# Where the weights of a decoder's first feed-forward are made ternary: in the cross-attention, or earlier, in the self-attention

## The chip, the cores and the metric

The kernel runs on one core of a Trainium2 chip. The metric is the device time of one execution in microseconds (us), the median of several runs. Five engines matter: PE (TensorE, the matrix multiplier, with its weight loads shown apart as PEld), DVE (VectorE), ACT (ScalarE), POOL (GpSimd), and SP (SyncE, which here only issues DMAs). Each works through its own queue in order: an instruction that waits holds up all that stand behind it on the same engine.

## The reference

Two decoder layers over x of shape (4, 512, 512), batch by batch. Each has a self-attention, a cross-attention and a feed-forward, and each of the six is followed by a sum with its input and a layer norm. What the change touches is the weight side of the first feed-forward:

```python
def weight_quant(w):
    scale = 1.0 / jnp.clip(jnp.mean(jnp.abs(w)), EPS)
    wq = jnp.clip(jnp.round(w * scale), -1.0, 1.0) / scale
    return w + jax.lax.stop_gradient(wq - w)
...
gate = bitlinear(x, w_gate)
up = bitlinear(x, w_up)
intermediate = jax.nn.silu(gate) * up
return h_bitlinear(intermediate, w_down)
```

So every weight becomes -1, 0 or 1 times a mean of absolute values over the whole matrix. That mean has to be known before the first weight can be rounded: each matrix (1 M weights, 4 MB) is read twice.

## The kernel before, in words

The six blocks are called A (self-attention), B (cross-attention), C (feed-forward) of layer 0, and D, E, F of layer 1; each has four batches, A0 to A3 and so on. `lanes` (L1254) runs two of them side by side: it takes one step of each in turn, and starts the next one when the last has said "next" and a lane is free. After each such round it gives one step to work in the background (`BESIDE`, L40): key C0 (`l0_ffn_scales`, L543) from the start of A1 to that of B0, key C (`l0_ffn_weights`, L575) from the start of B0 to that of B3. What the background hasn't done when a block needs it is done there at once (`need`, L1247).

`Pipe` (L43) puts an instruction off by some steps: `pipe.later(3, f)` calls f at the third `pipe.tick()` from now. The program is written in the order of these steps, and the framework's scheduler makes of it one queue for each engine: in the order of the code where nothing has to wait, ahead of it where an instruction is ready before others. `issue_after(ins)` (as in L557) keeps what is written under it behind `ins` on the queue of that instruction's engine; it is no wait at run time.

Buffers in SBUF are tiles of 128 partitions x 2 KB, in rings: O with 69 slots (most operands that live long: the high and low halves of the split float32 matrices, the exponentials, the ternary weights `tb`), T with 13, X with 12, W with 4 (weights on their way in, `tw`). PSUM has 8 banks.

**A (L330).** For each batch, q and k are projected (8 groups of 12 matmuls, "qk"), ACT adds the bias (`evac`, L340), DVE and POOL turn them by the rotary angles (`turn`, L349 and L352; `join`, L357), and they are split into a high and a low half (`split`, L137: the high one on ACT, L143, the low one on DVE or POOL, L146). Meanwhile the x of the next batch is loaded transposed and split, with the low halves `xTl` on POOL (`load_pairs`, L258). Then come v, the scores ("as"), the softmax, the transposes and the product with v ("pv"). POOL adds the bias row `bvo` to the four tiles of x (L408), which are needed only at the end, at L425.

**B (L457).** Per batch 16 steps. A step takes two heads: 6 matmuls for scores (L526), a row maximum on DVE (L474), an exponential on ACT (L476), a norm on POOL (L482), and six steps later 8 transposes (L248), copies (L489), and 4 matmuls into the output (L498).

**C0, beside A.** For each of the three matrices (`wg_t`, `wu_t`, `wd_t`) 16 chunks of 128x512 are loaded (256 KB each) and DVE sums their absolute values (`absum`, L558). A matmul adds these up over the partitions (L569), and L571 and L572 make the mean and the scale.

**C, beside B.** All 48 chunks are loaded again. For each, DVE does two instructions, `quant`: scale and add a large constant, which rounds (L587), and clip (L588). ACT then takes the constant off and writes bfloat16 (`put`, L596), two chunks to one tile `tb` of O. Gate and up come first, column group by column group, then down. From there C's matmuls (L687, L689, L741) read them.

Of the kernel before, what the change touches and what calls it, by code (L numbers as in the profile page):

```python
# [10 lines left out]
F32 = mybir.dt.float32  # L11
F32R = mybir.dt.float32r
F16 = mybir.dt.float16
BF16 = mybir.dt.bfloat16
I32 = mybir.dt.int32
U8 = mybir.dt.uint8
AF = mybir.ActivationFunctionType
ALU = mybir.AluOpType
AX = mybir.AxisListType
PSUM = bass.MemoryType.PSUM  # L20

B, S, D = 4, 512, 512
P = 128
NT = 4
MAGIC = 12582912.0
# [17 lines left out]
class Pipe:  # L43


    def __init__(self):
        self.todo = []
# [21 lines left out]
class Net:  # L69
    def __init__(self, ctx, tc, args):  # L70
        self.tc = tc
        self.nc = tc.nc
        self.a = args
        self.n = 0
        pool = lambda name, **kw: ctx.enter_context(tc.tile_pool(name=name, **kw))
        self.const = pool("const", bufs=1)
        self.op = pool("op", bufs=O_BUFS)
        self.tp = pool("tp", bufs=T_BUFS)
        self.xp = pool("xp", bufs=X_BUFS)
        self.wp_ = pool("wp", bufs=W_BUFS)  # L80
        self.small = pool("small", bufs=4)
        self.psum = pool("psum", bufs=8, space=PSUM)
        nc = self.nc
        tc.keep_in_program_order(nc.scalar.preload_act_table_set(LOG_EXP))
        self.ident = self.c("ident", [P, P])
        make_identity(nc, self.ident)
        self.ident16 = self.c("ident16", [P, P], BF16)
        nc.vector.tensor_copy(self.ident16, self.ident)
        self.ones = self.c("ones", [P, P])
        nc.gpsimd.memset(self.ones, 1.0)  # L90
        scratch = lambda name, shape: nc.dram_tensor(name, shape, F32, kind="Internal").ap()
        self.had_scratch = scratch("had_scratch", (2, NT, 2048, P))
        self.gu_codes = scratch("gu_codes", (22, P, 512))
        self.xd = [args["x"]] + [scratch(f"x{i}", (B, S, D)) for i in range(1, 6)] + [args["out"]]
        self.bg, self.table, self.emitted, self.piece, self.since = {}, None, {}, {}, {}

        self.low, self.stacked = {}, None
        self.gu, self.dn = {}, []
        self.pre = {}
        self.w1 = {}  # L100
        self.mean, self.scale = {}, {}
        self.tern = {name: {} for name in self.TERNARY}
# [227 lines left out]
    def l0_attn(self, b):  # L330
        nc, a = self.nc, self.a
        pipe = Pipe()
# [4 lines left out]

        def evac(ps, w, m):
            z = zs[w, m] = self.t("z")
            nc.scalar.activation(z, ps, AF.Identity, bias=self.qkb[:, w * NT + m : w * NT + m + 1], scale=1.0 if w else P ** -0.5)  # L340
            if m % 2:
                pipe.later(1, turn, w, zs[w, m - 1], z)

# [16 lines left out]
        for w in range(2):  # L360
            for m in range(NT):
                pipe.tick()
                ps = self.pa("qk")
                self.mm3(ps, [(self.cols(self.wqk[w][k], slice(m * P, (m + 1) * P)), xT[k]) for k in range(NT)])
                pipe.later(1, evac, ps, w, m)
                yield
            if b == 0 and w == 0:
                self.l0_attn_bv()
                yield from self.l0_attn_wvo(pipe)
# [16 lines left out]
        with self.tc.issue_after(self.pre.pop(("x", b)).ins):  # L386
            x = self.load_x(0, b)
# [4 lines left out]
        q, k = qk  # L392
        joined = self.joined
# [9 lines left out]
        for i in range(NT):  # L403
            pipe.tick()
            ps = self.pa("as")
            self.mm3(ps, [(self.cols(q[m], slice(i * P, (i + 1) * P)), k[m]) for m in range(NT)])
            with self.tc.issue_after(joined.ins):
                nc.gpsimd.tensor_tensor(x[i], x[i], self.bvo, ALU.add)  # L408
            pipe.later(1, soft, ps, i)
            yield  # L410
# [129 lines left out]
        w = self.a[name]  # L540
        return [(k, c, w[k * P : (k + 1) * P, c * 512 : (c + 1) * 512]) for c in range(w.shape[1] // 512) for k in range(w.shape[0] // P)]

    def l0_ffn_scales(self):  # L543

        nc = self.nc
        self.had = self.c("had", [P, P], F32R)
        self.had16 = self.load(self.c("had16", [P, P]), self.a["had16"])
        f = self.t("had")
        nc.gpsimd.dma_start(f[:, 0:P], self.a["had"])
        pipe = Pipe()  # L550
        pipe.later(3, nc.vector.tensor_copy, self.had, f[:, 0:P])
        for name in self.TERNARY:
            chunks = self.ternary_chunks(name)
            part = self.c(name + "_abs", [P, len(chunks)])

            def absum(f, n):
                with self.tc.issue_after(self.mark.ins):  # L557
                    nc.vector.tensor_reduce(part[:, n : n + 1], f, AX.X, ALU.add, apply_absolute_value=True)  # L558

            for n, (k, c, ap) in enumerate(chunks):  # L560
                pipe.tick()
                pipe.later(1, absum, self.load(self.w("tw"), ap), n)
                yield
            yield from pipe.drain()
            m = self.c(name + "_mean", [P, 4])
            nc.vector.tensor_reduce(m[:, 2:3], part, AX.X, ALU.add)
            yield
            ps = self.pb("tot")
            nc.tensor.matmul(ps[:, 0:1], self.ones, m[:, 2:3], start=True, stop=True)  # L569
            yield  # L570
            nc.vector.tensor_scalar(m[:, 0:1], ps[:, 0:1], 1.0 / (len(chunks) * P * 512), 1e-5, ALU.mult, ALU.max)  # L571
            nc.vector.reciprocal(m[:, 1:2], m[:, 0:1])  # L572
            self.mean[name], self.scale[name] = m[:, 0:1], m[:, 1:2]

    def l0_ffn_weights(self):  # L575

        nc = self.nc
        yield from self.bg["C0"]
        pipe = Pipe()
        order = [("wg_t", x) for x in self.ternary_chunks("wg_t")]  # L580
        up = [("wu_t", x) for x in self.ternary_chunks("wu_t")]
        order = [e for c in range(4) for e in order[4 * c : 4 * c + 4] + up[4 * c : 4 * c + 4]]
        order += [("wd_t", x) for x in self.ternary_chunks("wd_t")]
        cur = []

        def quant(name, k, c, f):
            nc.vector.tensor_scalar(f, f, self.scale[name], MAGIC, ALU.mult, ALU.add)  # L587
            nc.vector.tensor_scalar(f, f, MAGIC + 1.0, MAGIC - 1.0, ALU.min, ALU.max)  # L588
            pipe.later(1, put, name, k, c, f)

        def put(name, k, c, f):
            if not cur:
                cur.append(self.o("tb", BF16, 1024))
            o = cur[0][:, 0:512] if len(cur) == 1 else cur[0][:, 512:1024]
            cur.append(o)
            nc.scalar.activation(o, f, AF.Copy, bias=-MAGIC)  # L596
            self.tern[name][k, c] = o
            if len(cur) == 3:
                cur.clear()

        for name, (k, c, ap) in order:
            pipe.tick()
            pipe.later(1, quant, name, k, c, self.load(self.w("tw"), ap))
            yield
        yield from pipe.drain()

# [674 lines left out]
def body(tc, args, phases=range(6)):  # L1281
    with ExitStack() as ctx:
        net = Net(ctx, tc, args)
        net.gamma = net.load(net.c("gamma", [P, 1]), args["gamma"].to_broadcast([P, 1]))
        if 0 in phases:
            net.l0_attn_weights()
        net.bg = {("B", 0): net.l0_xattn_ctx(0), "C0": net.l0_ffn_scales(), "C": net.l0_ffn_weights(), "D": net.l1_attn_weights(), "F0": net.l1_ffn_codes(), "F": net.l1_ffn_weights()}
        f = [net.l0_attn, net.l0_xattn, net.l0_ffn, net.l1_attn, net.l1_xattn, net.l1_ffn]
        plain = ORDER.replace("+", "").replace("!", "").split()
        order = ORDER.split() if len(phases) == 6 else ["ABCDEF"[p] + str(b) for p in phases for b in range(B)]  # L1290

        def step(n):
            if len(phases) == 6:
                for first, last, key in BESIDE:
                    if plain.index(first) < n <= plain.index(last) + 1:
                        next(net.bg[key], None)

        def start(name):
            return f["ABCDEF".index(name[0])](int(name[1]))

        lanes(order, start, step)
# [68 lines left out]
```

## Time and profile before

| | us |
|---|---|
| three runs, median (lowest to highest) | 1584.54 (1584.25 to 1585.16) |
| the profiled execution, its own time | 1581.65 |
| its span, first to last instruction | 1580.0 |
| A, until B's first scores | 0 to 242.5 |
| B's scores, 64 steps | 242.5 to 445.5 |
| C, from its first gate matmul | from 461.6 |
| the loads of `tw` for C0 and C | 22.8 to 399.4 |
| `quant` on DVE | 229.8 to 409.4 |

| stretch, us | PE busy | DVE | ACT | POOL | DMA share |
|---|---|---|---|---|---|
| 0 to 242 | 233.8 | 161.9 | 93.1 | 144.1 | 0.43 |
| 242 to 461 | 212.6 | 201.3 | 182.5 | 112.4 | 0.38 |
| 461 to 765 | 293.2 | 231.8 | 240.9 | 98.9 | 0.50 |

How to read it: the first table says when each block runs, the second how long each engine was busy in these stretches (the third row is C). Matmuls are pipelined and their ends are modelled, so PE's figure is an upper one. The profile also has a list of groups of instructions, by line, engine and tile, with the busy time, the mean time of one in ns, and what ended the idle time before them; lists of who waited for whom; and the chain of work that ended last: from the last instruction it goes back, at each step to what released it or to the instruction before it on its engine.

### The profile page before, as it was taken

How to read it: one execution, taken by the hardware profiler on the slowest of the kernel's cores; microseconds unless marked ns; L12 is line 12 of the kernel's file. 1: busy time of each engine (PE TensorE's matmuls, PEld its weight loads, DVE VectorE, ACT ScalarE, POOL GpSimd, SP SyncE). 2: the span in 40 equal slices, each digit the busy share in tenths (PEclk: the TensorE clock that was granted, in tenths of full speed). 3: DMA queues.
4: the chain of work that ended last, by engine and by line, in shares of the span. 5: the costliest groups of instructions: out<-in, count | busy, mean ns of one | idle time of the engine just before them, and what ended most of it. 6: DMA issues, size and time to landing. Idle time of an engine off the chain costs nothing.

```text
span 1580.0 us, 25595 instructions
## 1 busy us (share of the span) xinstructions
PE 1515.4 (96%) x8222; PEld 1090.1 (69%) x8222; DVE 1232.9 (78%) x2658; ACT 1021.3 (65%) x2208; POOL 666.2 (42%) x672
## 2 busy tenths in 40 slices
PE   8999999999999999899999999999999999999996
PEld 6888786444544674477777668777687777777875
DVE  6486589999976688777577797767786888888896
ACT  5333336988878877888696864969634445545554
POOL 6673663555535303430435323353225344344342
PEclk9999999999999999999999999999999999999998
DMA  7043344455214744653434445633436630020101
GB/s 255 29 157 124 113 154 132 149 173 176 78 48 123 224 137 133 201 185 134 134 102 118 104 141 148 171 97 92 125 123 222 233 110 12 24 81 1 54 1 53
DMA packets 134150, 192.31 MB, mean 122 GB/s; under 512 B 17265, under 2 KB 52081, under 8 KB 134017
## 3 DMA queue, kind: packets, MB, share of 16 engines
q1 hardware_dynamic: 129888, 182.23, 36.3%
q0 software_dynamic: 4128, 8.46, 2.2%
q8 instruction: 65, 1.06, 0.3%
q14 instruction: 69, 0.56, 0.1%
HBM read 117.75 MB, written 47.71 MB: 105 GB/s over the span
## 4 chain that ended last, share of the span: by engine, by line
PE 63%; DVE 17%; ACT 8%; issue 6%; DMA 3%; POOL 3%; SPq 0%; ACTq 0%; DVEq 0%; POOLq 0%
PE fg L1185 7%; PE facc L1168 5%; PE dT L933 3%; DVE fg L1141 3%; PE pg L687 3%; PE had L755 2%; PE dn L741 2%; DVE bsm L474 2%; PE pu L689 2%; ACT de L923 2%; PE bo L498 2%; PE do L953 2%; PE qk L156 2%; PE qk L155 2%; PE qk L154 2%
## 5 line engine op out<-in xcount | busy, mean ns | idle before, releaser
L1141 DVE SCALAR_TENSOR_TENSOR fg<-fg,gs,fg 128x512 f32<-128x512 f32 x220 | 163.2, 745 | 30.9 <-ACT fg L1133 15.3
L923 ACT ACTIVATE de<-de,dm 128x128 f32<-128x128 f32 (+3 forms) x256 | 142.9, 563 | 11.3 <-DVE dm L919 10.9
L1185 PE MATMUL fg<-fxh,gu 128*128 128x512 f32 x352 | 140.2, 398 | 6.1 <-DVE fg L1141 3.1
L919 DVE CUSTOM_DVE_ANT_0 de<-ds,negm,thr 128x128 f32<-128x128 f32 (+3 forms) x256 | 126.4, 546 | 19.4 <-PE ds L908 16.0
L482 POOL TENSOR_SCALAR be<-be,bsm 128x512 f32<-128x512 f32 x128 | 96.5, 766 | 103.8 <-DVE bsm L480 72.7
L1185 PE MATMUL fg<-fxl,gu 128*128 128x512 f32 x352 | 137.4, 390 | 0.1
L664 POOL TENSOR_TENSOR hl<-g,hh 128x512 fp32r<-128x512 f32 x64 | 83.4, 1309 | 110.2 <-ACT hh L663 90.2
L1145 POOL TENSOR_TENSOR fg<-fg,fg 128x512 f32<-128x512 f32 x44 | 60.2, 1367 | 139.6 <-DVE fg L1141 60.0
L476 ACT ACTIVATE be<-bs,bsm 128x512 f32<-128x512 f32 x128 | 87.3, 690 | 31.1 <-DVE bsm L474 29.2
L845 POOL TENSOR_TENSOR dql<-dqf,dqh 128x512 fp32r<-128x512 f32 x32 | 41.4, 1295 | 150.8 <-ACT dqh L844 150.6
L933 PE MATMUL dT<-ident,de 128*128 128x128 f32 x640 | 92.0, 280 | 8.5 <-ACT de L923 6.4
L933 PEld LDWEIGHTS dT<-ident,de 128*128 128x128 f32 x640 | 72.3, 142 | 28.3 <-ACT de L923 14.0
L1185 PEld LDWEIGHTS fg<-fxh,gu 128*128 128x128 f32 x352 | 66.0, 188 | 30.1 <-DVE fg L1141 12.7
L474 DVE TENSOR_REDUCE bsm<-bs 128x1 f32<-128x512 f32 x128 | 83.4, 672 | 0.0
L498 PE MATMUL bo<-bpT,cT 128*64 128x512 f32 x256 | 76.7, 618 | 2.4 <-ACT bpT L489 1.2
L248 PEld LDWEIGHTS bT<-ident,be 128*128 128x128 f32 x512 | 54.9, 141 | 34.0 <-issue 11.5
L248 PE MATMUL bT<-ident,be 128*128 128x128 f32 x512 | 73.2, 281 | 3.6 <-POOL be L482 2.1
L1185 PEld LDWEIGHTS fg<-fxl,gu 128*128 128x128 f32 x352 | 66.1, 188 | 12.8 <-DVE fxl L146 0.4
L352 POOL TENSOR_TENSOR z<-z,rope_cos 128x512 f32<-128x512 f32 x32 | 46.8, 1473 | 64.8 <-DVE zs L349 57.8
L1133 ACT ACTIVATE fg<-fg,gs 128x512 f32<-128x512 f32 x88 | 60.1, 684 | 20.6 <-PE fg L1185 20.4
L687 PE MATMUL pg<-qT,tb 128*128 128x512 bf16 x256 | 66.8, 381 | 4.5 <-ACT qT L649 2.8
L1159 POOL TENSOR_TENSOR fhl<-fg,fhh 128x512 fp32r<-128x512 f32 x44 | 58.5, 1331 | 29.5 <-ACT fhh L1158 29.3
(355 smaller groups left out, 4640.3 us busy)
## 6 DMA issues: line engine op xcount, KB each, us to landing
x<-x SPq DMA_DIRECT2D x176, 256.0 KB, 3.0
had_scratch<-hw SPq DMA_DIRECT2D x64, 256.0 KB, 2.3
z<-had_scratch SPq DMA_DIRECT2D x64, 256.0 KB, 5.8
stk<-dqh SPq DMA_DIRECT2D x192, 64.0 KB, 2.1
tw<-in_wg_t SPq DMA_DIRECT2D x32, 256.0 KB, 3.8
tw<-in_wu_t SPq DMA_DIRECT2D x32, 256.0 KB, 3.7
tw<-in_wd_t SPq DMA_DIRECT2D x32, 256.0 KB, 2.8
p<-in_gu_p SPq DMA_DIRECT2D x22, 256.0 KB, 3.1
```

The costliest lines, as they stand in the source:

```text
L248: self.nc.tensor.transpose(pt[:, i * P : (i + 1) * P], srcs[i][:, j * P : (j + 1) * P], self.ident)
L474: nc.vector.tensor_reduce(sm[:, h : h + 1], ps, AX.X, ALU.max, negate=True)
L476: nc.scalar.activation(e, ps, AF.Exp, bias=sm[:, h : h + 1], accum_out=sm[:, 2 + h : 3 + h])
L482: nc.gpsimd.tensor_scalar(es[h][i], es[h][i], sm[:, 4 + h : 5 + h], 1.0, ALU.mult, ALU.mult)
L498: nc.tensor.matmul(po[0][h * 64 : h * 64 + 64, :], cT[j][:, c : c + 64], pTs[h], start=j == 0, stop=j == NT - 1)
L664: nc.gpsimd.tensor_tensor(lo, g, hi.bitcast(F32), ALU.subtract)
L687: nc.tensor.matmul(pg, tern["wg_t"][k, c][:, m], qT[k], start=k == 0, stop=k == NT - 1)
L919: nc.vector.tensor_tensor_reduce(es[i], ps, self.negm[:, 384 - P * i :], -1.0, self.thr[:, i : i + 1], ALU.add, ALU.min, n4[:, i : i + 1])
L923: nc.scalar.activation(es[i], es[i], AF.Exp, bias=n4[:, i : i + 1], scale=-1.0, accum_out=den[:, hh * 4 + i : hh * 4 + i + 1])
L933: nc.tensor.transpose(pt[:, o + (i - j) * P : o + (i - j + 1) * P], es[i][:, j * P : (j + 1) * P], self.ident)
L1141: self.emitted["DVE"] = nc.vector.scalar_tensor_tensor(y[u], ps, s, y[u], ALU.mult, ALU.add)
L1185: nc.tensor.matmul(ps, self.gu[i, u][:, g * P : (g + 1) * P], xT[g][n], start=n == 0, stop=n == 1)
```

## The change

- `l0_ffn_scales` becomes `l0_ffn_ternary`. While C0 sums up `wu_t`, it loads the 16 chunks of `wg_t` a second time, into tiles of O (`tq`), four steps ahead of their use, and makes them ternary; while it sums up `wd_t` it does so with `wu_t`. The work of one chunk is now: scale and round on ACT, one step later the clip on POOL, three steps later the bfloat16 on ACT into `tb`. Five steps after a pair is complete, SP stores its tile (256 KB) in DRAM (`tern_kept`). `issue_after` keeps the ACT work behind the latest `evac` written so far (`self.turned`), and the clip behind the latest `join`.
- `l0_ffn_weights` makes only `wd_t` ternary, still by two instructions on DVE and one on ACT, one chunk in three steps, and beside each chunk loads one of the 16 kept tiles back into a `tb`.
- C0 no longer empties its pipe between two matrices: it has 54 steps up to the last sum, and some ten more that empty the pipe.
- A's sums of x and `bvo` (L408) are queued behind the latest low half that POOL has been given, as well as behind the latest `join`.

```diff
-            with self.tc.issue_after(joined.ins):
+            with self.tc.issue_after(joined.ins), self.tc.issue_after(self.low[True].ins):
                 nc.gpsimd.tensor_tensor(x[i], x[i], self.bvo, ALU.add)
...
+        def quant(n, f):
+            if early:
+                with self.tc.issue_after(self.turned.ins):
+                    nc.scalar.activation(f, f, AF.Copy, bias=MAGIC, scale=self.scale[name])
+                pipe.later(1, clip, n, f)
+            else:
+                nc.vector.tensor_scalar(f, f, self.scale[name], MAGIC, ALU.mult, ALU.add)
+                nc.vector.tensor_scalar(f, f, MAGIC + 1.0, MAGIC - 1.0, ALU.min, ALU.max)
+                pipe.later(1, put, n, f)
+        def clip(n, f):
+            with self.tc.issue_after(self.joined.ins):
+                nc.gpsimd.tensor_scalar(f, f, MAGIC + 1.0, MAGIC - 1.0, ALU.min, ALU.max)
+            pipe.later(3, put, n, f)
+        def put(n, f):
+            if n % 2 == 0:
+                cur.append(self.o("tb", BF16, 1024))
+            o = cur[0]
+            with self.tc.issue_after(self.turned.ins):
+                nc.scalar.activation(o[:, n % 2 * 512 : n % 2 * 512 + 512], f, AF.Copy, bias=-MAGIC)
+            if n % 2:
+                cur.clear()
+                done(n // 2, o)
...
+        def keep(name, n, o):
+            pipe.later(5, lambda: nc.sync.dma_start(self.tern_kept[name][n], o.bitcast(F32)))
+        old = None
+        for new in self.TERNARY:
...
+            for n in range(len(chunks)):
                 pipe.tick()
-                pipe.later(1, absum, self.load(self.w("tw"), ap), n)
+                pipe.later(1, absum, self.load(self.w("tw"), chunks[n][2]), part, n)
+                if old:
+                    pipe.later(4, quant, n, self.load(self.o("tq"), todo[n][2]))
                 yield
...
     def l0_ffn_weights(self):
...
+        order = [(name, n) for c in range(0, 8, 2) for name in self.TERNARY[:2] for n in (c, c + 1)]
+        quant = self.ternary(pipe, "wd_t", lambda n, o: use("wd_t", n, o))
+        for n, (name, m) in enumerate(order):
+            pipe.tick()
+            pipe.later(1, quant, n, self.load(self.w("tw"), self.ternary_chunks("wd_t")[n][2]))
+            yield
+            pipe.tick()
+            o = self.o("tb", BF16, 1024)
+            self.load(o.bitcast(F32), self.tern_kept[name][m])
+            use(name, m, o)
+            yield
             yield
```

More of the change, by code (lines that the diff above doesn't have):

```diff
@@ L93, in __init__ @@
         self.gu_codes = scratch("gu_codes", (22, P, 512))
+        self.tern_kept = {name: scratch(name + "_kept", (8, P, 512)) for name in self.TERNARY[:2]}
         self.xd = [args["x"]] + [scratch(f"x{i}", (B, S, D)) for i in range(1, 6)] + [args["out"]]
@@ L339, in evac @@
             z = zs[w, m] = self.t("z")
-            nc.scalar.activation(z, ps, AF.Identity, bias=self.qkb[:, w * NT + m : w * NT + m + 1], scale=1.0 if w else P ** -0.5)
+            self.turned = nc.scalar.activation(z, ps, AF.Identity, bias=self.qkb[:, w * NT + m : w * NT + m + 1], scale=1.0 if w else P ** -0.5)
             if m % 2:
@@ L541, in ternary_chunks, with ternary, l0_ffn_ternary @@
         return [(k, c, w[k * P : (k + 1) * P, c * 512 : (c + 1) * 512]) for c in range(w.shape[1] // 512) for k in range(w.shape[0] // P)]
-    def l0_ffn_scales(self):
+    def ternary(self, pipe, name, done, early=False):
+        nc = self.nc
+        cur = []
+        def quant(n, f):
[20 more added lines that the diff above has]
+                done(n // 2, o)
+        return quant
+    def l0_ffn_ternary(self):
         nc = self.nc
@@ L551, in l0_ffn_scales, with absum @@
         pipe.later(3, nc.vector.tensor_copy, self.had, f[:, 0:P])
[L552 to L560, printed above, removed]
+        def absum(f, part, n):
+            with self.tc.issue_after(self.mark.ins):
+                nc.vector.tensor_reduce(part[:, n : n + 1], f, AX.X, ALU.add, apply_absolute_value=True)
+        def keep(name, n, o):
+            pipe.later(5, lambda: nc.sync.dma_start(self.tern_kept[name][n], o.bitcast(F32)))
+        old = None
+        for new in self.TERNARY:
+            chunks = self.ternary_chunks(new)
+            part = self.c(new + "_abs", [P, len(chunks)])
+            if old:
+                quant = self.ternary(pipe, old, lambda n, o, name=old: keep(name, n, o), early=True)
+                todo = self.ternary_chunks(old)
+            for n in range(len(chunks)):
                 pipe.tick()
-                pipe.later(1, absum, self.load(self.w("tw"), ap), n)
+                pipe.later(1, absum, self.load(self.w("tw"), chunks[n][2]), part, n)
+                if old:
+                    pipe.later(4, quant, n, self.load(self.o("tq"), todo[n][2]))
                 yield
-            yield from pipe.drain()
-            m = self.c(name + "_mean", [P, 4])
+            pipe.tick()
+            m = self.c(new + "_mean", [P, 4])
             nc.vector.tensor_reduce(m[:, 2:3], part, AX.X, ALU.add)
             yield
+            pipe.tick()
             ps = self.pb("tot")
@@ L570, in l0_ffn_scales, with use @@
             yield
+            pipe.tick()
             nc.vector.tensor_scalar(m[:, 0:1], ps[:, 0:1], 1.0 / (len(chunks) * P * 512), 1e-5, ALU.mult, ALU.max)
             nc.vector.reciprocal(m[:, 1:2], m[:, 0:1])
-            self.mean[name], self.scale[name] = m[:, 0:1], m[:, 1:2]
+            self.mean[new], self.scale[new] = m[:, 0:1], m[:, 1:2]
+            old = new
+        yield from pipe.drain()
     def l0_ffn_weights(self):
-        nc = self.nc
         yield from self.bg["C0"]
         pipe = Pipe()
[L580 to L601, printed above, removed]
-            pipe.tick()
-            pipe.later(1, quant, name, k, c, self.load(self.w("tw"), ap))
+        def use(name, n, o):
+            for h in range(2):
+                k, c, _ = self.ternary_chunks(name)[2 * n + h]
+                self.tern[name][k, c] = o[:, h * 512 : h * 512 + 512]
+        order = [(name, n) for c in range(0, 8, 2) for name in self.TERNARY[:2] for n in (c, c + 1)]
+        quant = self.ternary(pipe, "wd_t", lambda n, o: use("wd_t", n, o))
+        for n, (name, m) in enumerate(order):
+            pipe.tick()
+            pipe.later(1, quant, n, self.load(self.w("tw"), self.ternary_chunks("wd_t")[n][2]))
+            yield
+            pipe.tick()
+            o = self.o("tb", BF16, 1024)
+            self.load(o.bitcast(F32), self.tern_kept[name][m])
+            use(name, m, o)
+            yield
             yield
@@ L1286, in body @@
             net.l0_attn_weights()
-        net.bg = {("B", 0): net.l0_xattn_ctx(0), "C0": net.l0_ffn_scales(), "C": net.l0_ffn_weights(), "D": net.l1_attn_weights(), "F0": net.l1_ffn_codes(), "F": net.l1_ffn_weights()}
+        net.bg = {("B", 0): net.l0_xattn_ctx(0), "C0": net.l0_ffn_ternary(), "C": net.l0_ffn_weights(), "D": net.l1_attn_weights(), "F0": net.l1_ffn_codes(), "F": net.l1_ffn_weights()}
         f = [net.l0_attn, net.l0_xattn, net.l0_ffn, net.l1_attn, net.l1_xattn, net.l1_ffn]
```

## The prediction

> **What bounds the kernel now.** I read the page first, then the busy times in stretches, then the chain of work that ended last inside them.
>
> ```profile
> PE 1515.4 (96%) x8222; PEld 1090.1 (69%) x8222; DVE 1232.9 (78%) x2658; ACT 1021.3 (65%) x2208; POOL 666.2 (42%) x672
> ```
>
> By this PE is the bound all along, with 65 us idle. In B that is not so. Busy times in five stretches (PE, PEld, DVE, ACT, POOL):
>
> ```profile
> 120.00:242.00 122.00, 119.90 (x549) 97.86 (x547) 84.50 (x146) 41.48 (x84) 64.73 (x48) 1.00 0.41 133
> 160.00:180.00 20.00, 18.24 (x77) 13.82 (x76) 13.41 (x19) 6.93 (x13) 16.24 (x12) 1.00 0.68 224
> 242.50:261.00 18.50, 18.48 (x94) 12.85 (x94) 16.77 (x37) 11.49 (x29) 5.88 (x8) 1.00 0.18 58
> 261.00:400.00 139.00, 133.48 (x760) 66.97 (x758) 135.89 (x298) 123.10 (x300) 79.83 (x97) 1.00 0.52 165
> 400.00:445.50 45.50, 44.95 (x272) 23.26 (x270) 40.33 (x90) 35.92 (x91) 23.52 (x34) 1.00 0.16 53
> ```
>
> The reader is to see the fourth and fifth row. From 261 to 400 DVE is busy for 135.9 of 139 us; from 400 on, when `quant` has ended, for 40.3 of 45.5. By the starts of the L526 matmuls the first stretch holds 42 of B's steps (261.0 to 400.0), 3.31 us each; the second holds 15 (400.0 to 445.5), 3.03 us each. The chain of work in the free stretch is PE alone:
>
> ```profile
> 413.13 0.89 PE bs L526 x6
> 414.02 1.02 PE bT L248 x8
> 415.04 1.01 PE bo L498 x4
> ```
>
> A step is 0.89 + 1.02 + 1.01 = 2.92 us of PE, and 3.31 are taken. So B loses 42 x 0.39 = 16.4 us behind DVE. [...] In A it is the other way round: from 120 to 242 PE is idle for 2.1 us, 1.8 of them between 160 and 180. There the chain runs through POOL:
>
> ```profile
> 164.25 1.48 POOL z L357
> 165.73 1.74 POOL x L408 x2
> 168.91 2.98 POOL x L408 x2
> 171.90 4.98 POOL xTl L146 x4
> ```
>
> PE then goes on with a q matmul at 176.9: the four sums stand ahead of the low halves that it waits for.
>
> **The change part by part.** The durations:
>
> ```profile
> L588 DVE TENSOR_SCALAR tw<-tw x48: 382/418/1372, 230.8 to 409.4; 128x512 f32<-128x512 f32 x48
> L596 ACT ACTIVATE tb<-tw 128x512 bf16<-128x512 f32 x48 | 29.2, 634 | 0.0
> L721 ACT ACTIVATE q2f<-q2f,am 128x512 f32<-128x512 f32 x64 | 43.7, 750 | 4.5 <-DVE am L712 3.7 <-DVE ln L175 0.6
> L482 POOL TENSOR_SCALAR be<-be,bsm 128x512 f32<-128x512 f32 x128 | 96.5, 766 | 103.8 <-DVE bsm L480 72.7
> ```
>
> *DVE in B.* Of the 135.9 us between 261 and 400, L587 and L588 take 38.9 in 79 instructions (busy time of `tw` on DVE there), 0.98 us a chunk. Without them 103.8 us remain (busy time of all others). The change keeps only `wd_t`: one chunk in three steps. C gets 48 rounds there (B0 to B3, 16 each); some ten go to emptying C0's pipe, so 12 or 13 chunks fall here, 13 x 0.95 = 12.3 us. New demand: 116.1 us in 42 steps, 2.76 a step, against PE's 2.92. In the free stretch DVE had 40.3 us in 15 steps, 2.69 a step, and a step took 3.03; before, the demand was 3.24 and a step took 3.31. Ends: 2.92 (all 16.4 us won) and 3.20 (only 4.6 won). I take 3.07, just over the free stretch, to whose demand the new one is nearest: 42 x 0.24 = **-10.1 us**. What is late next is PE itself.
>
> *ACT and POOL in B.* ACT loses two thirds of its 25.5 us of `put` there, some 17 us; POOL gains nothing but the last three clips. ACT is not the bound (123.1 of 139): in the sum nothing. In 242.5 to 261 DVE has 1.3 us of `quant` in its chain (three instructions, the busy time of `tw`), which go; some 8 ACT instructions of `wu_t`'s tail (8 x 0.7 = 5.6 us beside 11.5 of 18.5 busy) come. Ends -1.3 and +2, taken as 0.
>
> *The sums of x.* Four sums (4.72 us) no longer stand before `xTl`: PE's wait of 1.76 us between 160 and 180 goes, with 3 us to spare for clips that fall there: **-1.8 us**. The sums are wanted only at L425, a softmax and four transposes later; their new place costs nothing as long as POOL gets round to them in those 20 us or so.
>
> *The work added to A.* 32 scalings on ACT by L721's 0.75 = 24 us, 32 puts by 0.634 = 20 us, 32 clips on POOL by 0.766 = 24.5 us, 32 loads and 16 stores of 256 KB on SP. `wu_t`'s summing, and with it the first `tq`, starts about 120 us in. So for 120 to 242: ACT 41.5 + 44 = 86 of 122 us, POOL 64.7 + 24.5 = 89, DVE as before. All of it lies beside PE's matmuls. What is queued behind it is what costs: behind a scaling or a put on ACT stand the next `evac`, the high halves and the exponentials, for 0.6 to 0.75 us each; behind a clip on POOL the next `join` and `xTl`, for 0.77; behind a store on SP, should its put be late, the loads of the next x. PE has other groups of the second lane in between, and eight PSUM banks. For DMA, 48 x 256 KB in some 125 us add 100 GB/s to the 133 of this stretch; 311 is the most that any slice of 20 us moved (0 to 20). Only in 160 to 180 (224 GB/s) do the two together exceed it.
>
> *Slots of O.* This is what no row shows. By the code A's fullest moment, the scores of A2 beside the projections of A3, holds 16 halves of wq and wk, 8 of wvo, 3 constants, 16 of q and k, 8 of v, 8 of xT: 59, and up to 4 exponentials, 63 of 69. A `tq` lives eight steps (4 + 1 + 3), so up to 8 live, and with a pair's five steps up to its store some 4 `tb`: 12 where 6 to 10 are free. Slots are handed out in the order of the code, so a load that finds none keeps a later exponential or high half waiting. Below: nothing, because instructions run as soon as their data is there and `tq` then lives shorter. Above: two such places, each short by up to 6 slots, with one freed a step of some 3 us: 18 us, less what PE bears (old rows: O is full at about 97 to 105 us, where no O tile is first written for 8 us, and PE stays busy), 10 us; two, 20 at the worst. I take **+1.5 us**, near the lower end, for the row where a full O cost PE nothing is the nearest.
>
> [...]
>
> *C and after.* Three or four chunks of `wd_t` and the kept tiles of the last column group are left to `need` at o = 12 of C0. Before, three chunks were left as well (last put at 524.5). Their loads have SP and DMA to themselves (0 GB/s in 440 to 460) and some 30 us; ends 0 and +4, the median landing of a `tw` load; taken as 0. From C on the code is the same, so what B wins is kept.
>
> **Sum:** -10.1 - 1.8 + 1.5 = -10.4 us. The profiled execution took 1581.65 (span 1580.0 and 1.65 around it): 1571.2. The median of the runs is 2.9 above it, so 1584.5 - 10.4 = **1574**.
>
> **The rivals.**
> *A stalls (slower).* Mechanism: O runs out between 135 and 190 us, the exponentials and high halves of A2 and A3 wait for slots, PE waits for them. Price as above, 10 to 20 us, with 15 in the middle: -10.1 - 1.8 + 15 + 2.5 (a load of x behind a blocked one, most of a landing) = +5.6, **1590**. It decides from 12 us of new PE idle time in A on. For it: 12 slots wanted, 6 to 10 free. Against: the 8 us at 97 to 105 without harm.
> *DVE stays the bound in B.* A share of 95% at PE's pace is much for one queue in order, and at the borders between batches (layer norm) a step takes up to 4.3 us even in the free stretch (400.0 to 404.3). Then 3.20 a step: -4.6 - 1.8 + 1.5, **1580**.
> [...]
> *A wash.* A loses some 9 us, what B gains: **1584**.
>
> **How the numbers follow.** Forecast (1571 to 1577.5) 0.42; PE's pace 0.13; DVE still bound 0.15; wash 0.10; A stalls 0.20. Faster 0.70, the same 0.10, slower 0.20, where 0.2% (3.2 us) is about what a measurement of this kernel can tell from no change. The range goes from 1566, which takes in most of PE's pace, to 1590, the middle of the stall: some 13% lie above and 5% below. The likeliest case's own range is 1571 to 1577.5.
>
> **What would show it.** In the profile after: L587 and L588 x16 each; DVE's share between the seventh and the 49th step of B near 90%, those steps at 3.0 to 3.15 us; no L408 ahead of `xTl` in the chain near 165; B's first scores at 241 to 243. I am wrong if they come later than 248, with PE's idle time in A put down to ACT, POOL or DMA behind `tq` and `tb`; or if B's steps stay above 3.2.

## The result, and the profile after

The changed kernel takes 1590.11 us (median of 6 runs, 1588.18 to 1591.71), beside 1584.39 for the kernel before on the same chip (6 runs): ratio 1.0038, 95% interval 1.0025 to 1.0052. It is slower by 0.4%, where 0.6% less was forecast. The profiled execution took 1590.18, with a span of 1588.5 (before: 1580.0). The first line of its page:

```profile
PE 1510.3 (95%) x8191; PEld 1091.2 (69%) x8222; DVE 1209.5 (76%) x2594; ACT 1041.7 (66%) x2240; POOL 684.5 (43%) x704
```

DVE is busy for 23 us less, as intended, and PE's idle time has grown from 65 to 78 us (a little of it only seemingly: 31 matmul records of C are missing in this profile). Busy times of the changed kernel in stretches, columns as in the prediction (PE, PEld, DVE, ACT, POOL, then the granted clock, the DMA share and GB/s); the third and fourth stretch are new, the fourth holds B's first six steps, the fifth the steps 7 to 48, the last the 15 after them:

```profile
120.00:242.00 122.00, 118.00 (x534) 96.27 (x533) 80.21 (x138) 67.39 (x127) 83.16 (x76) 1.00 0.67 210
160.00:180.00 20.00, 19.09 (x83) 15.19 (x82) 14.04 (x22) 15.41 (x31) 19.18 (x18) 1.00 0.79 250
240.00:260.00 20.00, 10.30 (x39) 7.16 (x39) 12.21 (x26) 16.44 (x35) 3.30 (x6) 0.66 0.67 223
253.70:274.80 21.10, 21.09 (x94) 13.78 (x94) 18.89 (x40) 13.88 (x33) 6.83 (x11) 0.90 0.15 51
274.80:402.50 127.70, 125.44 (x757) 65.49 (x756) 112.90 (x241) 108.27 (x270) 77.30 (x96) 1.00 0.43 145
402.50:447.80 45.30, 44.83 (x274) 23.32 (x272) 38.08 (x84) 35.77 (x91) 23.29 (x33) 1.00 0.19 65
```

The fifth row is the gain: 42 steps in 127.7 us, 3.04 each, where 3.31 were needed, and DVE at 88% where it was at 98%. The third row is the loss: PE is busy for 10.3 of 20 us, at a granted clock of 0.66. The same stretch before:

```profile
240.00:260.00 20.00, 19.32 (x100) 13.40 (x100) 17.46 (x38) 12.99 (x33) 5.88 (x8) 1.00 0.29 93
```

The first two rows are much as forecast: until some 239 us the work added to A lies beside PE, which was idle for 0.9 us between 160 and 180, where it had been for 1.8.

| stage | before, us | after, us | difference |
|---|---|---|---|
| start to A3's first scores | 220.5 | 219.9 | -0.6 |
| A3's first scores to B's ("the tail") | 22.0 | 33.8 | +11.8 |
| B's first six steps | 18.5 | 21.1 | +2.5 |
| B's steps 7 to 48 | 139.0 | 127.8 | -11.2 |
| the rest of B, to C's first gate matmul | 61.6 | 61.2 | -0.3 |
| C, to D's first projection ("dq") | 291.3 | 297.3 | +6.0 |
| the rest | 827.1 | 827.4 | +0.3 |

The tail took back all that B won. The chain of work there, in order of time (start, duration, what):

```profile
225.40 5.02 POOL x L410 x4
230.43 4.25 DMA tq<-in_wu_t
...
234.76 0.10 ACT tq L555
...
236.53 0.67 ACT ae L401 x2
237.19 0.11 ACT ln L224
...
238.72 1.76 DVE x L236 x3
240.48 0.03 SPq L239
...
240.59 4.99 DMA tq<-in_wu_t
245.58 0.02 issue
245.61 0.72 ACT tq L555
246.33 0.68 ACT ae L401 x2
247.00 0.04 issue
247.05 0.47 PE ap L249
```

(L410 is the sums of x, L555 the early scaling, L401 A's exponential, L224 and L236 layer norm, L239 the store of x1.) Read from the top: POOL makes the four sums. After them the bias row `bvo` is not needed any more, and its place in O goes to the tenth chunk of `wu_t`, whose load has stood at the head of SP's queue. It lands 4.25 us later; only then can ACT scale it, and behind the scaling stand the exponentials of A3 and the layer norm. DVE waits for the norm, SP for DVE's normed x, and behind that store stands a later load of `wu_t` (the fourteenth chunk), for which ACT waits again. PE's transposes begin at 247. The waits between 215 and 262 us (who, for whom: us in total, times, the longest):

```profile
ACT tq L555 <- DMA tq<-in_wu_t: 16.8, 7, 10.5
PE ap L249 <- ACT ae L401: 7.2, 3, 4.0
DVE ln L175 <- ACT ln L225: 7.0, 1, 7.0
```

SP's own waits between 200 and 260 us:

```profile
SPq L253 <- DVE wd_t_abs L592: 12.1, 8, 6.8
SPq L253 <- POOL x L410: 5.6, 1, 5.6
```

O was not full: by the tiles' addresses and the trace 52 to 57 of its 69 slots were in use at 225 to 230. Slots are given out in the order of the code, and this load had been given one that came free late. But the slot is only about half of ACT's 10.5 us. ACT was ready for the tenth chunk at 224.2. SP came to its load at 224.8, since it had stood before for places in W (the first row: loads of `tw` that wait for DVE's sums); then it stood 5.6 us for the slot, and the load took 4.25 to land. With the slot free at once, ACT would still have waited for some 5 us (an estimate from these times).

### The profile page after: what moved, and what is told of

It reads as the page before. It is cut to its first block, busy times and chain, and to the rows that moved or that the text cites. A ratio compares the mean times of both kernels' runs of the same rounds, so it can differ in the third digit from the quotient of the medians.

```text
span 1588.5 us, 25656 instructions
## 1 busy us (share of the span) xinstructions
PE 1510.3 (95%) x8191; PEld 1091.2 (69%) x8222; DVE 1209.5 (76%) x2594; ACT 1041.7 (66%) x2240; POOL 684.5 (43%) x704
## 4 chain that ended last, share of the span: by engine, by line
PE 60%; DVE 14%; ACT 9%; issue 6%; DMA 5%; POOL 4%; SPq 0%; ACTq 0%; DVEq 0%; POOLq 0%
PE fg L1227 7%; PE facc L1210 5%; PE dT L975 3%; DVE fg L1183 3%; PE bo L500 2%; PE bT L249 2%; ACT de L965 2%; PE dn L783 2%; PE bs L528 2%; PE do L995 2%; PE had L797 2%; PE pu L731 2%; PE pg L729 2%; PE ds L950 2%; PE qk L157 2%
## 5 line engine op out<-in xcount | busy, mean ns | idle before, releaser
L484 POOL TENSOR_SCALAR be<-be,bsm 128x512 f32<-128x512 f32 x128 | 93.6, 744 | 87.0 <-DVE bsm L482 62.7
L1175 ACT ACTIVATE fg<-fg,gs 128x512 f32<-128x512 f32 x88 | 60.1, 683 | 20.6 <-PE fg L1227 20.4
L500 PE MATMUL bo<-bpT,cT 128*64 128x512 f32 x256 | 71.5, 618 | 1.9 <-ACT bpT L491 1.0
L797 PE MATMUL had<-had,z 128*128 128x128 f32 x512 | 67.0, 280 | 5.2 <-DMA z<-had_scratch 5.1
L1201 POOL TENSOR_TENSOR fhl<-fg,fhh 128x512 fp32r<-128x512 f32 x44 | 58.5, 1330 | 29.6 <-ACT fhh L1200 29.4
L1179 ACT ACTIVATE fg<-fg,gs 128x512 f32<-128x512 f32 x44 | 30.3, 689 | 62.0 <-PE fg L1227 61.9
```

The source lines that it names most:

```text
L484: nc.gpsimd.tensor_scalar(es[h][i], es[h][i], sm[:, 4 + h : 5 + h], 1.0, ALU.mult, ALU.mult)
L500: nc.tensor.matmul(po[0][h * 64 : h * 64 + 64, :], cT[j][:, c : c + 64], pTs[h], start=j == 0, stop=j == NT - 1)
L797: nc.tensor.matmul(ps[:, c * P : (c + 1) * P], z[i * 4 + g][:, c * P : (c + 1) * P], self.had16, start=True, stop=True)
```

## The experiments

Every run is compared with the kernel before on its own chip. The table gives, for each, the ratio in its 95% interval, and from one profiled execution the start of A3's scores, the tail, B's first scores, a step of B (the mean of 7 to 48), and C; all in us.

| kernel | ratio (interval) | A3 | tail | B's first | step | C |
|---|---|---|---|---|---|---|
| before | 1 | 220.5 | 22.0 | 242.5 | 3.31 | 291.3 |
| the change | 1.0038 (1.0025 to 1.0052) | 219.9 | 33.8 | 253.7 | 3.04 | 297.3 |
| sums early | 1.0084 (1.0072 to 1.0096) | 225.0 | 34.6 | 259.6 | 3.04 | 294.7 |
| sums alone | 0.9989 (0.9979 to 1.0000) | 219.0 | 21.2 | 240.2 | 3.32 | 291.8 |
| bias row in its own place | 1.0039 (1.0026 to 1.0052) | 221.0 | 30.1 | 251.1 | 3.03 | 292.4 |
| gate only | 0.9977 (0.9968 to 0.9987) | 220.4 | 21.1 | 241.4 | 3.18 | 293.8 |
| gate, half of up | 1.0013 (1.0004 to 1.0023) | 220.8 | 29.6 | 250.4 | 3.13 | 292.0 |
| scaling on POOL | 1.0044 (1.0027 to 1.0061) | 223.3 | 29.0 | 252.3 | 3.03 | 295.8 |
| started 10 rounds earlier | 1.0006 (0.9995 to 1.0017) | 231.7 | 20.9 | 252.6 | 3.05 | 291.6 |
| PE kept busy | 1.0043 (1.0029 to 1.0056) | 219.5 | 33.5 | 253.0 | 3.06 | 291.0 |
| half of up, bias row in its own place | 0.9982 (0.9972 to 0.9992) | 219.8 | 24.0 | 243.8 | 3.18 | 293.6 |
| bias row, stored one step behind | 1.0019 (1.0007 to 1.0030) | 220.0 | 28.9 | 248.9 | 3.05 | 292.1 |
| started 4 rounds earlier | 1.0006 (0.9996 to 1.0015) | 228.0 | 25.5 | 253.5 | 3.05 | 292.7 |
| nine places of their own | 1.0042 (1.0027 to 1.0058) | 228.5 | 26.9 | 255.4 | 3.03 | 291.2 |
| eleven places of their own | 1.0007 (0.9998 to 1.0016) | 226.9 | 21.9 | 248.8 | 3.02 | 295.0 |

My first theory (K below) was that the bias row's slot, set free late by the moved sums, costs the tail; the rival W, that it is the early work as such.

**1. The sums of x back in their old place**, the rest of the change kept:

```
-            with self.tc.issue_after(joined.ins), self.tc.issue_after(self.low[True].ins):
+            with self.tc.issue_after(joined.ins):
```

> The changed kernel with the sums of x and the bias row queued as before (behind the latest join alone). Theory K (a knot of queues: in A3 a load of a quarter tile of wu_t stands on SP until the four sums of A3 have freed the slot of the bias row, which they now do behind the low halves of the context; ACT waits 10.5 us for that load, A3's exponentials stand behind it, PE idles 10.5 us in pieces and its clock is halved for 13.7 us): the slot is free some 8 us earlier, ACT's longest wait for a tq load falls to 4 us or less, no halved clock at the start of B, B's first scores at 242 to 246 instead of 253.7; C's second loss (6 us) may stay or go. 1577 to 1584. Rival W (32 more scalings, clips and puts in A's queues cost by their amount, wherever the sums stand): first scores at 250 or later, 1587 to 1592.

It was the slowest of all. The bias row's slot, free at 233.8, now went to a high half of B's k (`kh`), for which ACT waited 7.92 us, until 233.9, and tq waits of 3.1 and 5.5 followed; with the sums ahead of the low halves A3's scores came 5 us later too. Theory K's number fell, and the loss was above what W gave it.

**2. The moved sums alone**, in the kernel before (the same line, the other way round).

> The kernel before with the sums of x behind the latest low half, and nothing else. Prediction's term: PE's wait of 1.8 us between 160 and 180 goes, 1582.6 against 1584.4. Theory K: no tq is there to take the slot of the bias row, so nothing is lost at A3's end either: 1581 to 1584.5. Rival S (the later sums themselves make A3 or B0 late): B's first scores later than 244, 1587 or more.

The step of the prediction holds as far as it can be measured: 0.11% is 1.7 us, against 1.8 forecast, in an interval that reaches from 0.2% down to nothing; and PE was busy for all 20 us between 160 and 180, where it had been for 18.24. Alone the move does no harm.

**3. The bias row in a place of its own**, the whole change otherwise:

```
-O_BUFS, T_BUFS, X_BUFS, W_BUFS = 69, 13, 12, 4
+O_BUFS, T_BUFS, X_BUFS, W_BUFS = 68, 13, 12, 4
...
-        self.bvo = self.o("bvo")
+        self.bvo = self.c("bvo", [P, 512])
```

> The changed kernel with the bias row in a place of its own and 68 slots in ring O instead of 69, sums behind the low halves as in the change. Theory K: no load can wait for the sums any more; ACT's longest wait for a tq load falls to 4 us or less, B's first scores at 242 to 246, 1577 to 1584. Rival W: first scores at 250 or later, 1587 to 1592. A third way: with one slot fewer another tile takes the place of the bias row and the stall moves.

K fell: 1.0039, no better. The tenth chunk now had the place of a ternary tile, stored at 223.0 and landed at 226.4; its own load came behind that and landed at 232.4, and ACT waited 7.4 us. What stays of K is a late slot, whichever it is, and even that not alone: SP stood only 1.0 us for this one.

**4. Only the gate early**; up and down on DVE beside B.

```
-            if old:
+            if old == "wg_t":
```

(and the same at the load, with 32 chunks left to C's rounds.)

> The changed kernel with only wg_t made ternary in A; wu_t and wd_t are made so on DVE in B, wg_t is loaded back beside wu_t. Theory K: no tq is under way at A3's end, B's first scores at 241 to 243, no halved clock there. DVE's work in B falls by a third of quant instead of two: steps 7 to 48 at about 3.2 us instead of 3.31 (3.04 in the change), 4 to 5 us. 1577 to 1582, more if C loses its 6 us here too. Rival W: half of A's loss, first scores at 247, 1585 to 1588.

As theory K said: no wait for a `tq` at the tail, steps of 3.18, and faster than the kernel before by 0.23%. It has the lowest ratio of all kernels here (the interval of run 9 overlaps). So 16 chunks of early work are no loss as such.

**5. The gate and half of up.**

```
-                if old:
+                if old == "wg_t" or old and n < 8:
                     pipe.later(4, quant, n, self.load(self.o("tq"), todo[n][2]))
```

(and 24 chunks left to C's rounds.)

> The changed kernel with only the first 8 of the 16 chunks of up made ternary in the self-attention; the last 8 and all of down are made ternary on DVE beside the cross-attention, so 24 chunks there where the changed kernel has 16 and the gate alone had 32. Theory T (only the chunks whose loads fall into the tail of the fourth batch cost; in the changed kernel chunks 1 to 9 had no long wait): no wait over 2 us of ACT for a tq load, no half clock near 244 us, first scores of the cross-attention at 241 to 243 us, steps 6 to 48 at about 3.11 us (between 3.04 and 3.175 measured), in all 1574 to 1578 us, the fastest so far. Theory W (every early chunk costs its share of the 11 us): first scores at 246 to 249 us, 1580 to 1585 us. Theory S (the last early load gets a late slot whichever it is): a wait of 5 us or more on ACT somewhere between 200 and 235 us, first scores from 247 us on.

None of the three as put: ACT had no wait for a `tq` of up, B's first scores came even later than W said (250.4), and the tail was still 7.6 us longer than before. Its chain of work (L253 on SP is a load, L558 the scaling on DVE):

```profile
226.34 5.56 POOL x L410 x4
...
231.92 0.33 SPq L253
...
232.34 4.69 DMA tw<-in_wu_t
237.02 0.03 issue
237.05 0.49 DVE tw L558
```

The same slot of the bias row had now gone to a load for B (`cT`). SP stood for it from 224.2 to 231.9, behind it stood the load of a `wu_t` chunk for DVE, and DVE, in order, stood 6.2 us for that. From the waits of SP (200 to 260), of DVE and of PE (215 to 262):

```profile
SPq L253 <- POOL x L410: 7.4, 1, 7.4
DVE tw L558 <- DMA tw<-in_wu_t: 6.2, 1, 6.2
PE ap L249 <- ACT ae L401: 6.1, 3, 3.9
```

**6. The scaling on POOL instead of ACT**, whole change.

```
-                with self.tc.issue_after(self.turned.ins):
-                    nc.scalar.activation(f, f, AF.Copy, bias=MAGIC, scale=self.scale[name])
+                with self.tc.issue_after(self.joined.ins):
+                    nc.gpsimd.tensor_scalar(f, f, self.scale[name], MAGIC, ALU.mult, ALU.add)
```

> The changed kernel with the early scaling on POOL (its clip's engine) instead of ACT; the puts stay on ACT. The loads stand on SP as before. Theory ACT (what carries the late load to PE is ACT's order: the exponentials and the Ln stand behind the scaling that waits): the wait moves to POOL, ACT's exponentials of the fourth batch come on time, first scores at 241 to 245 us, in all 1577 to 1583 us. Theory any engine (POOL has the input sums, the low halves of k for the first scores and the clips in order behind the same load, and gets some 20 us of work more): first scores at 248 us or later, a POOL wait of 5 us or more for a tq load between 220 and 240 us, in all 1587 to 1596 us.

The wait went with the instruction, as "any engine" said; between 215 and 262 us:

```profile
POOL tq L555 <- DMA tq<-in_wu_t: 7.9, 2, 6.0
PE bs L528 <- ACT qh L471: 5.6, 1, 5.6
```

**7. All of it 10 rounds earlier**, from the ninth of the first batch's 18 rounds (`EARLY` is 8):

```
...
+            if n == 1 and len(rounds) > EARLY:
+                next(net.bg["C0"], None)
```

> The changed kernel with the absolute sums and the ternary work behind them started in the first batch (from the ninth round) and not with the second, so that everything of it comes some 10 rounds earlier and the 10th chunk of up is loaded near 195 us and not at 230. Theory T (the place: the loads that fall into the tail of the fourth batch): no ACT wait over 2 us for a tq load between 215 and 245 us, first scores of the cross-attention at 241 to 244 us, steps 6 to 48 at 3.04 us, in all 1574 to 1579 us. Rival (the slots of O and the queues of the first batches are full, the loss only moves): PE idle time of several us between 60 and 200 us, the fourth batch's scores begin at 224 us or later instead of 219.9, in all 1583 us or more.

The tail's loss is gone (20.9 us) and the rival is right all the same: 11 us are lost before A3. Load after load of `tw` stood on SP for a place in W that DVE's sums set free, the last until 111.2; behind them came a `tq` load that landed at 115.3, ACT waited 6.8 us for it, and PE had gaps of 2.95 and 2.61 us at 124 and 127.

**8. PE kept busy through its gaps**: 24 matmuls that nobody reads, 16 before and among A3's first transposes, 8 ahead of B's first scores. The line that issues one of them:

```
+            self.warmed = self.nc.tensor.matmul(self.idle[:, 0:P], self.ident, self.ident, start=True, stop=True)
```

> The changed kernel with 24 matmuls of 128x128 of the identity by itself, into a tile that nobody reads, on PE alone: 16 before the first transposes of the fourth batch's probabilities and among them, 8 ahead of the first scores of the cross-attention, where PE stood idle for 1.7, 1.4, 4.0 and 3.3 us. Theory clock (the halved clock from 244.4 to 258.0 us costs time of its own: the 16 transposes and the scores run at half speed and end later): no half clock there, the sixth step of the cross-attention at 270 to 272.5 us instead of 274.8, in all 1586 to 1588 us. Rival (PE waits for ACT and DVE there anyway, the clock is a mark and no cost): sixth step at 274 to 276 us, in all 1589 to 1591.5 us.

Between the two. The stretch from 240 to 260:

```profile
240.00:260.00 20.00, 13.11 (x82) 10.36 (x83) 11.27 (x24) 15.29 (x33) 3.12 (x5) 0.91 0.64 213
```

The clock is 0.91 there instead of 0.66 (by that mean, half for 3.4 to 3.8 us of the 20, where it was 13.65 from 244.4), and B's seventh step starts 1.7 us earlier (273.1 for 274.8), 0.7 of it because B itself began so much earlier. In all nothing is won (1.0043). So here the halved clock came with the stall, and was a small part of its price: 1.0 us of those 1.7, beside the 11.8 of the tail.

**9. Half of up, with the bias row in its own place**: the edits of 5 and 3 together.

> The gate and half of up early, as before, and the bias row of the input sums in a place of its own, with O at 68 slots. In the run with half of up SP stood from 224.2 to 231.9 us for the bias row's slot, with a load for the cross-attention, and behind it came the load that DVE waited 6.2 us for. Theory knot (one load that stands on SP for a late slot holds every load behind it, and with them an engine that takes its work in order): with that slot gone SP does not stand over 3 us between 220 and 240, DVE does not wait for a load of up, first scores of the cross-attention at 241 to 244 us, steps 6 to 48 at 3.1 us, in all 1573 to 1577 us. Rival (the next load in the row stands for another late slot, as when the bias row was moved in the whole change): first scores at 247 us or later, in all 1579 to 1584 us.

The theory of the knot holds in its main point. Against run 5 one tile was moved (and, since O has one slot less, the places of others with it), and B's first scores came at 243.8 instead of 250.4, and the ratio went from 1.0013 to 0.9982, with intervals apart. DVE waited for no load of up there, and PE's wait at the tail shrank to this:

```profile
PE ap L249 <- ACT ae L401: 1.2, 2, 0.9
```

One sign was missed: SP did stand for more than 3 us between 220 and 240, 5.7 us for a put, but no load that an engine waited for stood behind it. The total came out above the forecast 1573 to 1577 (1580.31, on a chip whose kernel before took 1583.37), since B's step was 3.18 and not 3.1.

**10. Run 3, and the tiles stored one step behind instead of five.**

```
-            pipe.later(5, lambda: nc.sync.dma_start(self.tern_kept[name][n], o.bitcast(F32)))
+            pipe.later(1, lambda: nc.sync.dma_start(self.tern_kept[name][n], o.bitcast(F32)))
```

> The whole change with the bias row in a place of its own (O at 68), and the ternary tiles stored one step after their put instead of five, so that their slots come free about four rounds earlier. With the bias row moved alone, the 10th load of up stood for a ternary tile that was stored at 223.0 and landed at 226.4, and ACT waited 7.4 us. Theory late slot: that slot is free by 218 us, the load lands by 224, ACT waits less than 3 us, first scores at 242 to 246 us, in all 1577 to 1583 us. Rival (the stores wait on SP for the puts instead, and hold the loads behind them, so that the wait only moves): first scores at 249 us or later, in all 1586 to 1592 us.

Halfway: ACT's longest wait went from 7.4 to 5.9 us, the tail from 30.1 to 28.9, the ratio from 1.0039 to 1.0019. SP stood 20.1 us for puts in 200 to 260, as the rival said. And this run shows what the slot is not: SP stood only 0.9 us for the place of the tenth chunk, whose load left at 225.3 and landed at 229.7, and ACT waited 5.9 us for it all the same. That part comes from SP being late with the load and from its landing, whatever the slot.

**11. All of it 4 rounds earlier** (run 7 with EARLY at 14).

> The changed kernel with the absolute sums and the ternary work started 4 rounds earlier, in the last 4 of the first batch's 18 rounds (10 rounds earlier the tail's stall was gone, but 10 us were lost near 95 to 130 us, where ACT waited 6.8 us for a tq load behind a load of up that stood for its slot). Theory place (the losses are knots at single places, and between them there is room): no ACT wait over 3 us for a tq load in the whole of A, the fourth batch's scores at 219 to 222 us, first scores of the cross-attention at 241 to 245 us, in all 1573 to 1579 us. Rival (the early work costs A its 10 us wherever it is put): first scores at 250 to 254 us, in all 1578 to 1590 us.

The rival: 7.5 us are lost before A3's scores and 3.5 in the tail, where SP stood 7.3 us for the bias row's slot again.

**12 and 13. `tq` in places of its own**: run 3, with the loads going round nine, then eleven places of O that they keep.

```
...
+                    own.append(self.o("tq") if len(own) < 9 else own[-9])
-                    pipe.later(4, quant, n, self.load(self.o("tq"), todo[n][2]))
+                    pipe.later(4, quant, n, self.load(own[-1], todo[n][2]))
```

> The whole change with the bias row in a place of its own (O at 68) and the loads of gate and up for the early pass going round nine places of O that they keep, so that none of them waits for a slot of another tile: each waits only for the put of the chunk nine before it. The kernels with the bias row moved waited 7.4 us (stores five behind) and 5.9 us (one behind) at the tail. Theory late slot (the wait at the tail is for a slot of another tile, given out far ahead): ACT waits less than 2 us for a load of up between 215 and 245, first scores of the cross-attention at 242 to 246 us, steps 6 to 48 at 3.04 us, the cross-attention's end some 6 us ahead of the kernel before, in all 0.2 to 0.5% under it. Rival (SP stands for the puts on ACT instead, since each load now waits for one, and holds the input and output of the batches behind it): SP waits of 5 us or more for a put, first scores at 249 us or later, in all 0.1 to 0.5% over the kernel before.

> The same with eleven places, so that a load waits for a put two rounds older, and O has two slots less for the rest. Theory late slot: as with nine, first scores at 242 to 246 us, in all 0.2 to 0.5% under the kernel before, and SP stands less for puts than with nine. Rival (O has no two slots to give: 68 of 69 are in use near 150 and 180 us): the scores of the third or fourth batch begin 3 us or more later, PE idle time near 150 or 180 us, in all no faster than the kernel before.

With nine the rival holds: ACT waits 10.0 us for `tq` loads, 4 times, because they now wait for its own puts. SP stood 9.2 us for these between 200 and 260, and A3's scores come 8.0 us late. With eleven the tail is as it was before the change (21.9), and B's step is 3.02; ACT still waits 4.0 us for `tq` loads, 3.1 at the longest, where the theory gave less than 2. But A3's scores come 6.4 us late, so that B begins no earlier than in run 10, and the loads of the tail have had more time: these two runs alone don't settle it, and the cleanest evidence for the late slot stays run 9 against run 5. For the rival, 68 of O's slots are in use from 180 to 190, and between 195 and 222 us

```profile
POOL z L353 <- DVE zs L350: 9.2, 3, 7.9
```

is the longest wait. Why DVE came late to that rotation I have not separated.

## Why the prediction was wrong

**Right:** what bounds B, and its gain. Steps of 3.04 us for 3.07, -11.2 us for -10.1; DVE's demand 112.9 us for 116.1. **Right:** the sums' own -1.8 (-1.7 alone, though the interval reaches nothing). **Right as far as it went:** the work added to A. Scaling, clip and put took 0.72, 0.62 and 0.62 us (0.75, 0.766 and 0.634 in the sum), and up to A3's scores nothing was lost.

**The step that failed** is "Slots of O", with the sentence ahead of it: "behind a scaling or a put on ACT stand the next `evac`, the high halves and the exponentials, for 0.6 to 0.75 us each". That is the price of an instruction that has its data. One that waits for a load holds everything behind it for as long as the load is late: 10.5 us once, 16.8 in all. Of the 10.5, 5.6 were the load's wait for its slot; the rest was SP, late with the load behind others, so that the four steps between load and use no longer covered its landing. I took +1.5, near the lower end of 0 to 20, because a full O at 97 to 105 had cost PE nothing; the tail alone was +11.8. That row was the wrong neighbour: there PE stayed busy behind the full ring, while at A3's end nothing else was ready for it, and it had 10.5 us of gaps.

The rival "A stalls" named O and gave 1590, which is what was measured, but not the place nor quite the way. It said O runs out between 135 and 190 us; there all 69 slots were in use from 149 to 153 and from 175 to 183, and PE was idle for only 0.9 us. The loss came at 224 to 254 with slots to spare, through one load's particular slot and SP's late turn. That its number fits is in part luck: it took +17.5 us for A and nothing for C, where the tail and B's first steps were +14.3 and C +6.0 in the profiled execution. What would show the forecast wrong was named rightly: first scores later than 248, with PE's idle time put down to ACT behind `tq`.

**"Their new place costs nothing"** held for the sums alone, not beside the rest. In the change they stand on POOL behind `kl` and five clips, end at 230.4, and with them the bias row's slot comes late. In run 5, where a load for B had this slot, moving the bias row (run 9) won 5.6 us of the tail and 6.6 of B's start.

**The stretch 242.5 to 261**, taken as 0, was +2.5: B's first steps at a granted clock of 0.90 in the mean. In run 8, with a mean of 0.91 from 240 to 260 where it was 0.66, they took 1.0 us less; the rest stays open.

**C**, taken as 0 with ends 0 and +4, was +6.0 in the one profiled execution: PE stood 4.5 us at 558.8 for a load of `z` (1.3 at the same place before). The same instructions of C took 291.0 to 292.7 in runs 3, 7, 8, 10, 11 and 12, and 294.7 to 295.8 in 1, 6 and 13, all with the whole change, against 291.3 before. So the change's work in C doesn't cost this by itself; where in time C's queues meet may, which no run tried by itself. What sets it stays open, and a part of the 8.5 us between the two spans belongs to single executions: the medians are 5.7 apart.

**Where the gain went**, then: won in B as forecast, and given back before it. Each cure of the tail moved the loss (to POOL, to SP, or to the batches before) as long as all 32 chunks were early. With 16, or with 24 and the bias row out of the way, the kernel is 0.2% faster than before.

## What to carry to other kernels

A load issued into a shared ring has a price that its duration doesn't show (here it landed in 4.25 us, and ACT stood for 10.5): who holds the slot it was given, what stands ahead of it and behind it on the loading queue, and what stands behind the instruction that wants it. Before work is moved to an engine with room, follow those three, above all at a point where PE has only one lane to draw on. And try half of the move: here the gate alone had half of B's gain (steps of 3.18 between 3.31 and 3.04) and met none of the waits.

## What the runs showed of the hardware

In the kernel before, PE's granted clock was 0.50 for 3.41 us from 1132.5; in the changed kernel for 13.65 us from 244.4, among the tail's gaps of 1.7, 1.4, 4.0 and 3.3 us, and for 6.83 from 561.9, inside the gap of 4.5 at 558.8 (both profiles also end at 0.50, from 1569.4 and 1579.1). At 0.50 a matmul of `pv` took 0.63 us (at 257.4) and eight of `had` 2.05 (at 563.4); at the full clock they took 0.39 (at 258.4) and 1.11 (at 570.8). In run 9 the mean from 338 to 346 was 0.79, with PE busy for 6.26 of these 8 us. How long a gap has to be isn't shown: in the kernel before, one of 1.89 at 498.1 left the clock at full, while gaps of 0.64, 0.16 and 0.74 lay just ahead of the half clock at 1132.5.

In the kernel before, DVE's clip of a chunk (L588) took 0.41 to 0.43 us in the 28 of 48 that met no instruction of POOL. All seven that took over 0.6 lay beside POOL's work, the longest with 1.37 at 340.1; others beside it took 0.38 to 0.42.

In the changed kernel, on POOL, a tensor_scalar of 128x512 with two constants (L564) took 0.617 us in the median, one with a scalar for each partition (L484) 0.696.
